# The recurrences of a four-layer kernel: LSTM products in four pieces, a new order of a step, weights split on other engines, and the adaptive part later

## The chip, the cores and the metric

The kernel runs on one core of a Trainium2 chip. Its time is the device time of one execution in microseconds; lower is better. The engines are named as in the profile: PE (TensorE, with PEld for its weight loads), DVE (VectorE), ACT (ScalarE), POOL (GpSimd) and SP (SyncE, which issues most DMAs).

## What is computed

The input x has 8 sequences of 512 positions and 256 features, and every sequence has a condition vector of 256. Four layers are added one after the other, each as a residual:

```
x = x + rnn(x, h0 = cond)                    # h = tanh(x_t Wx + b + h Wh)
x = x + lstm(x, h0 = cond)                   # a = x_t Wx + b + h Wh  (4 x 256 columns)
                                             # i, f, o = sigmoid(a0), sigmoid(a1), sigmoid(a2); g = tanh(a3)
                                             # c = f * c + i * g;  h = o * tanh(c)
x = x + transformer_block(x, cond)           # hyperbolic attention and feed forward,
                                             # shift and scale from ada = cond @ w_ada + b_ada (6 x 256)
x = x + experts(x, cond)                     # 4 experts, the 2 best of a sequence, and a shared one
```

The first two layers are recurrences of 512 steps each. The change lies in them and in what is done beside them: the adaptive product `ada`, and the splitting of the later layers' weights into two parts.

## The kernel before

**The recurrences.** `recurrences` runs both of them in one loop of 520 iterations: in iteration `it` the RNN makes step r = it and the LSTM step l = it - 8, whose input is the RNN's output. PE, ACT and DVE run this loop in the order in which it is written (`manual_schedule`), POOL and SP are scheduled by the framework. Four steps make a quad (G = 4), and s below is the step's place in its quad. All 8 sequences go through a step together, as columns of the stationary operand (8 to 32 of them, as the quad fills up), and the weights are the moving operand, in fp32. The output features lie in four tiles of 32 partitions (Q = 4): `tiles4` issues one product for each, so that a call is four matmuls of the language and, in fp32, eight records of the profile.

**PSUM.** For each of the two alternating quads there are four banks: `pR` holds the RNN's sums (64 columns), and three pieces of `pL` hold the LSTM's 256 columns: 128 columns (f of both halves of the features, i and g of the first half), 64 columns (i and g of the second half), and 64 columns (o). ACT copies the bias into a bank of the coming quad (L391, L402), PE adds the inputs' products (`rnn_inputs`, `lstm_inputs`, spread by `lstm_plan`), and each step adds the products with h (`rnn_mm`, `products`).

**A step of the LSTM** (`lstm_step`): PE makes the first piece, DVE turns it (L476), ACT takes the tanh (L477); likewise the second piece (L481, L482); DVE makes f * c (L483); the third piece is turned (L486) and gets its tanh (L487); DVE scans the first half of the features (L466), ACT takes its tanh (L491), and the same for the second half; DVE multiplies by o (L493) and so writes the h that the next step's products load. Sigmoids are made from tanh.

**A step of the RNN**: `rnn_mm` (PE), a transpose (L434, DVE), a tanh into the slot of h (L435, ACT). In an iteration it stands behind the LSTM's step.

Beside the steps, once per quad: `rnn_add` (L441) adds the RNN's output to x, `turn_x` (L261) turns a quad of x, `lstm_add` (L449) forms the sum that is later stored.

**Weights.** `split_weights` (L178 to L210) makes 44 pieces of 128 x 512: POOL issues the load (L186), copies to fp32r (L188), subtracts (L189) and issues the store of both parts to DRAM (L191, L193). It is called ahead of the loop.

**The adaptive part** (`adaptive`, L499 to L511) makes ada = cond @ w_ada + b_ada in three blocks of 512 columns on PE, spread over the first seven iterations; the results use the banks of the second quad's three pieces. The load of `w_ada` is issued on ACT's queue behind the recurrences' weights (L291).

**After the recurrences** a transformer and experts part follows, in an order that a planner with a cost table makes when the program is built (all its instructions are recorded under L1624). It begins when the last store of the LSTM's output is read back.

Of the kernel before, what the change touches and what calls it, by code (L numbers as in the profile page):

```python
# [11 lines left out]
F32 = mybir.dt.float32  # L12
F32R = mybir.dt.float32r
AF = mybir.ActivationFunctionType
ALU = mybir.AluOpType
# [36 lines left out]
def body(ctx, tc, a, out):  # L52
# [19 lines left out]
    with tc.tile_pool(name="split", bufs=2) as sp:  # L72
        recurrences(
            tc, a, ident, ones, xd, ada_d, condT, ctx, lambda: split_weights(nc, a, sp, sd),
            lambda: constants(nc, a, sp, ident, ones, condT, consts),
        )
# [101 lines left out]
def split_weights(nc, a, pool, sd):  # L178


    G = nc.gpsimd

    def split(n, src):
        name = "_".join(map(str, n))
        raw = pool.tile([P, 2, D], F32, tag="raw", name=f"raw_{name}")
        G.dma_start(raw, src)  # L186
        t = pool.tile([P, 2, 2, D], F32R, tag="parts", name=f"parts_{name}")
        G.tensor_copy(t[:, 0], raw)  # L188
        G.tensor_tensor(t[:, 1], raw, t[:, 0].bitcast(F32), ALU.subtract)  # L189
        if len(n) == 3 and n[0] != E:  # L190
            G.dma_start(sd[n[1:]][n[0] * P : (n[0] + 1) * P], t)  # L191
        else:
            G.dma_start(sd[n], t)  # L193

    def columns(w, q=0):
        return w.rearrange("(c p) g -> p c g", p=P)[:, :, q * D : (q + 1) * D]

    def row_chunks(w, q):
        return w.rearrange("(m p) g -> p m g", p=P)[:, 2 * q : 2 * q + 2, :]

    for n in "qkvo":
        split(n, columns(a[f"L2_cond_w_{n}"]))
    for i in (E, 0, 1, 2, 3):
        w1, w2 = (a[f"L3_cond_sw{k}"] if i == E else a[f"L3_cond_ew{k}"][i] for k in (1, 2))
        for q in range(4):
            split((i, 1, q), columns(w1, q))
            split((i, 2, q), row_chunks(w2, q))


def recurrences(tc, a, ident, ones, xd, ada_d, condT, manual, load_next, constants):  # L210
# [16 lines left out]
    with ExitStack() as ctx:  # L227
# [63 lines left out]
        nc.scalar.dma_start(w_ada, a["L2_cond_w_ada"].rearrange("(c p) g -> p c g", p=P))  # L291
        nc.scalar.dma_start(b_ada, a["L2_cond_b_ada"].rearrange("(o g) -> o g", o=1))
        ada = one.tile([B, 6 * D], F32, name="ada")
        load_next()
# [18 lines left out]
        def set_h(n, q):  # L313
            o = (q % 2) * SET
            return slots[n][:, o + 8 : o + 8 + SET].rearrange("p (u x) -> p u x", x=2 * S + 8)


        bank_R = [ps.tile([P, 512], F32, name=f"pR{i}") for i in range(2)]
        pR = [t[:, : DC * S].rearrange("p (c s) -> p c s", c=DC) for t in bank_R]
        pieces = ((0, 4 * S), (4 * S, 6 * S), (6 * S, 8 * S))  # L320
        bank_L = [[ps.tile([P, 512], F32, name=f"pL{n}{i}") for n in range(3)] for i in range(2)]
        pL = [[bank_L[i][n][:, : hi - lo] for n, (lo, hi) in enumerate(pieces)] for i in range(2)]
# [53 lines left out]
        def open_bank(t, row_of):  # L376
            for j in range(Q):
                nc.tensor.matmul(
                    t[32 * j : 32 * j + 32], lhsT=ones[0:1, :32], rhs=row_of(j), start=True, stop=True, skip_group_check=True
                )  # L380
# [4 lines left out]
        def rnn_inputs(q, i):  # L385

            o = pR[q % 2]
            if i == 0 and q < 2:
                open_bank(o, lambda j: row0.rearrange("p (c j s) -> p c j s", c=DC, j=Q)[:, :, j, :])
            elif i == 0:  # L390
                nc.scalar.copy(flat(o), b0)  # L391
            else:
                k = i - 1
                tiles4(o, XL[:, k, G * q : G * q + G, :].rearrange("p t b -> p (t b)"), w0_cols(wx0, k), False, False)

        def lstm_inputs(q, i, piece):
            lo, hi = pieces[piece]
            o = pL[q % 2][piece]
            if i == 0 and q < 2:
                open_bank(o, lambda j: row1[:, j, lo:hi])  # L400
            elif i == 0:
                nc.scalar.copy(o, b1[:, lo:hi])  # L402
            else:
                k = i - 1
                tiles4(o, XL[:, k, G * q : G * q + G, :].rearrange("p t b -> p (t b)"),
                       lambda j: lw["x"][:, k, j, lo:hi], False, False)


        lstm_plan = [[(0, 0), (0, 1), (0, 2)], [(1, 0), (1, 1)], [(1, 2), (2, 0)], [(2, 1), (2, 2)]]
# [27 lines left out]
        def rnn_add(q):  # L437

            for c in range(DC):
                x = XL[:, c, G * q : G * q + G, :]  # L440
                V.tensor_tensor(x, x, set_h(0, q)[:, :, c * S : c * S + 8], ALU.add)  # L441
# [4 lines left out]
        def lstm_add(q):  # L446
            at = slice(G * q, G * q + G)
            for c in range(DC):
                V.scalar_tensor_tensor(  # L449
                    XT[:, c, :, at].rearrange("p b t -> p t b"),  # L450
                    set_h(1, q)[:, :, c * S : c * S + 8], 0.5, XL[:, c, at, :], ALU.mult, ALU.add,
                )

        def lstm_step(t, between):
# [5 lines left out]
            def products(piece):  # L460
                lo, hi = pieces[piece]
                for k in range(DC):
                    tiles4(pre[piece], h[:, k, : 8 * tt + 8], lambda j: lw["h"][:, k, j, lo:hi], False, tt == G - 1 and k == 1)
# [7 lines left out]
            def tile_of(blocks, tag):  # L471
                return sp.tile([P, blocks, S], F32, tag=tag, name=f"{tag}_{t}")

            products(0)
            f = tile_of(4, "f")
            V.transpose(flat(f), pre[0])  # L476
            nc.scalar.activation(dd[:, 0:4, :, 2], f[:, :, rows], AF.Tanh, scale=0.5)  # L477
            products(1)
            between()
            g = tile_of(2, "g")  # L480
            V.transpose(flat(g), pre[1])  # L481
            nc.scalar.activation(dd[:, 4:6, :, 2], g[:, :, rows], AF.Tanh, scale=0.5)  # L482
            V.scalar_tensor_tensor(dd[:, 2:6:2, :, 3], dd[:, 0:2, :, 2], 1.0, sc_old[:, :, :, 3], ALU.add, ALU.mult)  # L483
            products(2)
            o, to = tile_of(2, "o"), sp.tile([P, DC, B], F32, tag="to", name=f"to_{t}")
            V.transpose(flat(o), pre[2])  # L486
            nc.scalar.activation(to, o[:, :, rows], AF.Tanh, scale=0.5)  # L487
# [11 lines left out]
        def adaptive(i):  # L499
            i, c = divmod(i, DC + 1)  # L500
            cols, pa = slice(512 * i, 512 * (i + 1)), bank_L[1][i][:B]
            if c < DC:
                nc.tensor.matmul(
                    pa, lhsT=condT[:, c, :], rhs=w_ada[:, c, cols], start=(c == 0), stop=False, skip_group_check=True
                )
                return
            nc.tensor.matmul(
                pa, lhsT=ones[0:1, :B], rhs=b_ada[:, cols], start=False, stop=True, skip_group_check=True
            )
            nc.scalar.copy(ada[:, cols], pa)  # L510
            nc.sync.dma_start(ada_d[:, cols], ada[:, cols])  # L511

        b0, b1 = (one.tile([P, n * S], F32, name=f"b{i}") for i, n in enumerate((DC, 8)))
        rnn_inputs(0, 0)
        nc.scalar.copy(b0, flat(pR[0]))
        for i in range(1, 3):
            rnn_inputs(0, i)
        parts = [lambda i=i: adaptive(i) for i in range(3 * (DC + 1))]
        for it in range(T + LAG):
            r, l = it, it - LAG  # L520
            if it == 1:
                turn_rows(XL[:, :, G : G * sizes[0], :], x_first[:, G:, :])
                prepare_bias()
                for piece, (lo, hi) in enumerate(pieces):
                    lstm_inputs(0, 0, piece)
                    nc.scalar.copy(b1[:, lo:hi], pL[0][piece])
            if 1 <= it < LAG:
                for _ in range(-(-len(prepare) // (LAG - it))):
                    prepare.pop(0)()

            def add():
                if r % G == 0 and 0 < r <= T:
                    rnn_add(r // G - 1)

            if l < 0:
                add()
            else:
                if l == 0:
                    for i, piece in sum(lstm_plan, []):
                        if i:  # L540
                            lstm_inputs(0, i, piece)
                lstm_step(l, add)
            if r in (T // 2, T - 3, T - 2):
                fill_constants(bank_R[NQ % 2])
            if r == G:
                fill_constants = constants()
            if 0 < l and l % G == 0:
                lstm_add(l // G - 1)
                if l % P == 0:
                    store(l - P, l)  # L550
            if r < T:
                rnn_mm(r)
                rnn_vec(r)
            if 0 <= l and l // G + 1 < NQ:
                for part in lstm_plan[l % G]:
# [1210 lines left out]
```

## Time and profile before

| | us |
|---|---|
| median of 3 runs | 2729.81 (2729.31 to 2731.14) |
| the profiled execution | 2732.08 |
| its span | 2730.3 |
| PE busy | 2123.2 (78%) |
| PEld busy | 1620.3 (59%) |
| DVE busy | 1957.5 (72%) |
| ACT busy | 1307.5 (48%) |
| POOL busy | 414.6 (15%) |

The span runs from the first to the last instruction of the profiled execution. Busy times are sums over a span with two parts that have different limits, so the share of an engine over the whole says little; stretches of the trace and single steps are read below. Lines such as L370 and L1624 are those of helpers: there the names of the tiles tell groups apart. In the group lines, the number behind x is a count, then come busy time and the mean duration of one in ns, and behind the bar the idle time of the engine just before.

### The profile page before, as it was taken

The page shows a single profiled execution, that of the slowest core. Times are in us where ns is not written, and L with a number is a line of the kernel's source. Part 1 is how long each engine was busy: PE and PEld are TensorE (multiplying, and loading weights), DVE is VectorE, ACT ScalarE, POOL GpSimd, SP SyncE. Part 2 cuts the span into 40 slices and gives each one's busy share as a digit, 9 for nine tenths or more (in the row PEclk, how much of TensorE's full clock was granted, in tenths as well). Part 3 has the DMA queues.
Part 4 walks back from the last instruction along what each step waited for, and adds up shares of the span by engine and source line. Part 5 has one row for each costly group of instructions (what it writes and reads, how often), then busy time and mean ns, then how long its engine had stood idle before and what let it go on. Part 6 is the DMA issues. An engine that isn't in the chain of part 4 may idle for free.

```text
span 2730.3 us, 112042 instructions
## 1 busy us (share of the span) xinstructions
PE 2123.2 (78%) x47067; PEld 1620.3 (59%) x47067; DVE 1957.5 (72%) x8931; ACT 1307.5 (48%) x5047; POOL 414.6 (15%) x467
## 2 busy tenths in 40 slices
PE   5667666766666677766577978889979898999699
PEld 4556656666656566665454444656648475667487
DVE  6776666666666666666565686987877788687884
ACT  2334445454544444444336855455564745564222
POOL 6770000000000000000022332131212222211000
PEclk8568999899999999899888768999989899999799
DMA  7550001000100001000241111433415243243364
GB/s 217 187 184 16 9 5 28 5 12 5 28 5 7 11 5 26 4 5 5 67 155 57 39 60 41 166 130 109 141 66 185 76 145 109 97 139 120 123 208 154
DMA packets 114771, 214.94 MB, mean 79 GB/s; under 512 B 42733, under 2 KB 67888, under 8 KB 114258
## 3 DMA queue, kind: packets, MB, share of 16 engines
q1 hardware_dynamic: 103048, 168.97, 19.0%
q0 software_dynamic: 9856, 34.61, 3.8%
q8 instruction: 369, 6.05, 0.9%
q10 hardware_dynamic: 1362, 4.20, 0.4%
q14 instruction: 136, 1.11, 0.1%
HBM read 167.85 MB, written 39.90 MB: 76 GB/s over the span
## 4 chain that ended last, share of the span: by engine, by line
PE 46%; DVE 30%; ACT 16%; issue 5%; DMA 1%; POOL 1%; SPq 0%; ACTq 0%; DVEq 0%; POOLq 0%
PE pL L370 13%; PE ph L1624 8%; PE py L1624 8%; PE sc L1624 5%; DVE f L476 5%; ACT scan_in L477 5%; PE po L1624 4%; DVE scan_in L483 4%; ACT to L487 4%; DVE slots_h L493 4%; DVE o L486 3%; ACT th L491 2%; PE pf L1624 2%; DVE h L1624 2%; ACT pL L402 1%
## 5 line engine op out<-in xcount | busy, mean ns | idle before, releaser
L370 PE MATMUL pL<-wh,slots_h 128*8 128x64 f32 (+2 forms) x24576 | 608.5, 251 | 409.6 <-DVE slots_h L493 408.5
L370 PEld LDWEIGHTS pL<-wh,slots_h 128*8 128x8 f32 (+1 forms) x24576 | 506.9, 106 | 503.9 <-DVE slots_h L493 492.2
L476 DVE STREAM_TRANSPOSE f<-pL 128x128 f32<-128x128 f32 x512 | 162.1, 317 | 231.8 <-PE pL L370 224.0
L1624 PE MATMUL py<-h,we 128*128 128x512 f32 x1152 | 301.6, 396 | 18.1 <-DVE h L1624 18.1
L1624 ACT ACTIVATE ex<-sc 128x512 f32<-128x512 f32 x512 | 269.0, 612 | 93.5 <-PE sc L1624 91.0
L1624 PE MATMUL ph<-xf,we 128*128 128x512 f32 x1152 | 301.9, 398 | 3.1 <-DVE o L1624 3.1
L477 ACT ACTIVATE scan_in<-f 128x32 f32<-128x32 f32 x512 | 133.8, 261 | 281.0 <-DVE f L476 275.9
L1624 PEld LDWEIGHTS py<-h,we 128*128 128x128 f32 x1152 | 214.6, 189 | 69.7 <-DVE h L1624 24.5
L1624 PEld LDWEIGHTS ph<-xf,we 128*128 128x128 f32 x1152 | 214.8, 190 | 51.8 <-issue 6.7
L370 PE MATMUL pR<-r_L_cond_Wh,slots_h 128*8 128x64 f32 (+3 forms) x8192 | 230.7, 230 | 3.5 <-issue 2.7
L435 ACT ACTIVATE slots_h<-r 128x16 f32<-128x16 f32 x512 | 110.5, 216 | 242.7 <-DVE r L434 242.7
L493 DVE SCALAR_TENSOR_TENSOR slots_h<-to,th 128x8 f32<-128x8 f32 x1024 | 148.7, 172 | 85.2 <-ACT th L491 85.0
L370 PE MATMUL pL<-wx,XL 128*32 128x64 f32 (+1 forms) x6144 | 207.5, 253 | 1.7 <-issue 1.1
L1624 PE MATMUL sc<-q_t,k_t 64*128 64x512 f32 x512 | 172.2, 527 | 28.9 <-ACT ex L1624 25.6
L483 DVE SCALAR_TENSOR_TENSOR scan_in<-scan_in,scan_out 128x16 f32<-128x16 f32 x512 | 125.6, 245 | 94.5 <-ACT scan_in L477 87.1
L466 DVE TENSOR_TENSOR_SCAN scan_out<-scan_in 128x32 f32<-128x32 f32 x1024 | 180.8, 216 | 0.0
L487 ACT ACTIVATE to<-o 128x16 f32<-128x16 f32 x512 | 110.4, 216 | 145.2 <-DVE o L486 127.9
L491 ACT ACTIVATE th<-scan_out 128x8 f32<-128x8 f32 x1024 | 161.4, 204 | 26.1 <-DVE scan_out L466 26.0
L370 PEld LDWEIGHTS pR<-r_L_cond_Wh,slots_h 128*8 128x8 f32 (+3 forms) x8192 | 162.9, 106 | 12.1 <-issue 7.8
L1624 ACT ACTIVATE g<-ph,b 128x512 f32<-128x512 f32 x128 | 87.9, 688 | 170.5 <-PE ph L1624 142.0
L1624 PEld LDWEIGHTS sc<-q_t,k_t 64*128 64x128 f32 x512 | 73.8, 211 | 151.4 <-ACT ex L1624 120.6
L1624 PE MATMUL po<-ex,v 128*32 128x512 f32 x1024 | 162.5, 685 | 0.4 <-ACT ex L1624 0.4
(396 smaller groups left out, 3683.4 us busy)
## 6 DMA issues: line engine op xcount, KB each, us to landing
we<-sde SPq DMA_DIRECT2D x128, 512.0 KB
we<-sd SPq DMA_DIRECT2D x64, 512.0 KB
sde<-parts POOLq DMA_DIRECT2D x32, 512.0 KB, 3.1
raw<-in_L_cond_ew POOLq DMA_DIRECT2D x32, 256.0 KB, 3.5
xT<-xd SPq DMA_DIRECT2D x16, 512.0 KB
sd<-parts POOLq DMA_DIRECT2D x8, 512.0 KB, 3.7
xd<-XT SPq DMA_DIRECT2D x4, 1024.0 KB
xtd<-x SPq DMA_DIRECT2D x8, 512.0 KB
```

The costliest lines, as they stand in the source:

```text
L370: nc.tensor.matmul(out[32 * j : 32 * j + m], lhsT=lhsT, rhs=rhs_of(j), start=start, stop=stop, skip_group_check=True)
L402: nc.scalar.copy(o, b1[:, lo:hi])
L435: nc.scalar.activation(slot_h(0, t + 1), r[:, :, 8 * tt : 8 * tt + 8], AF.Tanh)
L466: V.tensor_tensor_scan(sc[:, c].rearrange("p b s -> p (b s)"), dd[:, 2 + 2 * c].rearrange("p b s -> p (b s)"), dd[:, 3 + 2 * c].rearrange( ...
L476: V.transpose(flat(f), pre[0])
L477: nc.scalar.activation(dd[:, 0:4, :, 2], f[:, :, rows], AF.Tanh, scale=0.5)
L483: V.scalar_tensor_tensor(dd[:, 2:6:2, :, 3], dd[:, 0:2, :, 2], 1.0, sc_old[:, :, :, 3], ALU.add, ALU.mult)
L486: V.transpose(flat(o), pre[2])
L487: nc.scalar.activation(to, o[:, :, rows], AF.Tanh, scale=0.5)
L491: nc.scalar.activation(th[c], sc[:, c, :, 3], AF.Tanh)
L493: V.scalar_tensor_tensor(out[:, c], to[:, c], 1.0, th[c], ALU.add, ALU.mult)
L1624: r = f(*args, **kw)
```

## The change

In the recurrences:

- The LSTM's sums lie in four pieces of 64 columns, one bank each: f of both halves, i and g of the first half, i and g of the second, o. `pR` moves into columns 64 to 128 of the fourth piece's bank. Each step issues the products of all four pieces in a row.
- DVE turns the four pieces one by one, and ACT takes one tanh per piece; f * c stands behind the third transpose, o's transpose behind f * c.
- An iteration begins with the RNN's transpose and tanh, and its products for the coming step stand at the end of the iteration. `rnn_add` (now one instruction), `turn_x` and `lstm_add` stand at s = 0, 1 and 2, between the RNN's transpose and the LSTM's first. ACT's bias copies stand two by two at s = 0 and 1, one ahead of the step's tanhs and one behind them.
- The weights are split in 88 halves of pieces, from the LSTM's third quad on, one per quad: ACT copies (`hi`) at the end of s = 2, DVE subtracts (`lo`) at s = 3. Loads and stores stay on POOL's queue.
- The load of `w_ada` is issued on POOL's queue at l = 4, and `ada` is made in six blocks of 256 columns in the LSTM's quads 95 to 100, in unused columns of the pieces' banks.

```diff
-        bank_R = [ps.tile([P, 512], F32, name=f"pR{i}") for i in range(2)]
-        pR = [t[:, : DC * S].rearrange("p (c s) -> p c s", c=DC) for t in bank_R]
-        pieces = ((0, 4 * S), (4 * S, 6 * S), (6 * S, 8 * S))
-        bank_L = [[ps.tile([P, 512], F32, name=f"pL{n}{i}") for n in range(3)] for i in range(2)]
+        NP = 4
+        bank_L = [[ps.tile([P, 512], F32, name=f"pL{n}{i}") for n in range(NP)] for i in range(2)]
+        pieces = tuple((2 * S * n, 2 * S * (n + 1)) for n in range(NP))
+        pL = [[bank_L[i][n][:, : 2 * S] for n in range(NP)] for i in range(2)]
+        pR = [bank_L[i][NP - 1][:, 2 * S : 4 * S].rearrange("p (c s) -> p c s", c=DC) for i in range(2)]
...
+    def hi(self):
+        i, c = self.jobs[0]
...
+        self.nc.scalar.copy(self.parts[i][:, 0, c], self.raw[i][:, c])
+
+    def lo(self):
+        i, c = self.jobs.pop(0)
+        t, n = self.parts[i], self.pieces[i][0]
+        self.nc.vector.tensor_tensor(t[:, 1, c], self.raw[i][:, c], t[:, 0, c].bitcast(F32), ALU.subtract)
+        if c == 0:
+            return
...
+        self.load(i + 2)
...
-            products(0)
-            f = tile_of(4, "f")
-            V.transpose(flat(f), pre[0])
-            nc.scalar.activation(dd[:, 0:4, :, 2], f[:, :, rows], AF.Tanh, scale=0.5)
-            products(1)
-            between()
...
+            for piece, (lo, hi) in enumerate(pieces):
+                for k in range(DC):
+                    tiles4(pre[piece], h[:, k, : 8 * tt + 8], lambda j: lw["h"][:, k, j, lo:hi], False, tt == G - 1 and k == 1)
+            for piece in range(3):
+                nc.scalar.activation(dd[:, 2 * piece : 2 * piece + 2, :, 2], turned(piece), AF.Tanh, scale=0.5)
             V.scalar_tensor_tensor(dd[:, 2:6:2, :, 3], dd[:, 0:2, :, 2], 1.0, sc_old[:, :, :, 3], ALU.add, ALU.mult)
...
+            to = sp.tile([P, DC, B], F32, tag="to", name=f"to_{t}")
+            nc.scalar.activation(to, turned(3), AF.Tanh, scale=0.5)
...
+            if r < T:
+                rnn_vec(r)
...
+            if s == 0 and 0 < r <= T:
+                rnn_add(rq - 1)
+            elif s == 1 and next_r:
+                turn_x(rq + 1)
+            elif s == 2 and l > 0:
+                if lq > 0:
+                    lstm_add(lq - 1)
...
+            elif s == 3 and split:
+                weights_split.lo()
+
+            if lq >= 1 and s < 2:
+                start_piece(lq + 1, 2 * s, next_l, next_r)
...
+            if l >= 0:
+                lstm_step(l)
+
+            if s < 2:
+                start_piece(lq + 1, 2 * s + 1, lq >= 1 and next_l, rq >= 1 and next_r)
+            if s == 2 and split:
+                weights_split.hi()
+
+            plan = ([(0, 0), (0, 1)], [(1, 0), (1, 1), (2, 0)], [(2, 1), (3, 0), (3, 1)], [])[s]
+            if next_l:
+                for part in plan:
+                    lstm_inputs(lq + 1, *part)
+            if s == 3 and next_r:
+                for k in range(DC):
+                    rnn_inputs(rq + 1, k)
+            if r + 1 < T:
+                rnn_mm(r + 1)
+            if ada_i is not None and s in (0, 2):
+                if s == 0:
+                    ada_row(ada_i)
+                ada_products(ada_i, s // 2)
...
+            if l == G:
+                V.memset(w_ada[:, 0, :1], 0.0)
+                nc.gpsimd.dma_start(w_ada, a["L2_cond_w_ada"].rearrange("(c p) g -> p c g", p=P))
...
-        for it in range(T + LAG):
-            r, l = it, it - LAG
...
-                lstm_step(l, add)
...
-            if r < T:
-                rnn_mm(r)
-                rnn_vec(r)
```

## The prediction

> **What bounds the kernel now.** I read the slices of the page first, then busy time by stretch, then the two stretches' instructions, then one step in order of time, last the chain of waits of the start.
>
> ```profile
> span 2730.3 us, 112042 instructions
> POOL 6770000000000000000022332131212222211000
> PEclk8568999899999999899888768999989899999799
> ```
>
> The recurrences fill the first half (their last result is at 1348.6 us); POOL works only in the first three of 40 slices there, and just there the TensorE clock is low. Stretches (PE, PEld, DVE, ACT, POOL busy, then clock, DMA share, GB/s):
>
> ```profile
> 60.00:200.00 140.00, 85.30 (x2700) 73.42 (x2692) 107.46 (x352) 44.95 (x234) 101.47 (x130) 0.62 0.56 186
> 200.00:1340.00 1140.00, 793.56 (x37333) 704.75 (x37333) 765.70 (x4904) 561.15 (x3268) 5.54 (x10) 0.96 0.05 11
> ```
>
> One instruction of L483 runs in each LSTM step, so its record counts steps (min/median/max ns, first and last start):
>
> ```profile
> L483 DVE SCALAR_TENSOR_TENSOR scan_in<-scan_in,scan_out x42: 140/561/1911, 33.2 to 203.9; 128x16 f32<-128x16 f32 x42
> L483 DVE SCALAR_TENSOR_TENSOR scan_in<-scan_in,scan_out x470: 146/190/196, 207.2 to 1347.6; 128x16 f32<-128x16 f32 x157
> ```
>
> 42 steps take (207.2 - 33.2) / 42 = 4.143 us each while POOL splits weights, 470 take (1347.6 - 207.2) / 469 = 2.432 after. The order of time in the slow phase shows why:
>
> ```profile
> 103.82 1.79 DVE L466 TENSOR_TENSOR_SCAN scan_out<-scan_in 128x32 f32<-128x32 f32 x2
> 104.12 1.28 POOL L189 TENSOR_TENSOR parts<-raw,parts 128x512 fp32r<-128x512 f32 x1
> 105.52 0.33 ACT L491 ACTIVATE th<-scan_out 128x8 f32<-128x8 f32 x2 [1.38 <-DVE scan_out L466]
> ```
>
> Two scans that end together after 0.30 us elsewhere last until POOL's instruction is over. Row by row between 60 and 206 us, 14 scans that overlap POOL's TENSOR_TENSOR have a median of 1890 ns; 37 that overlap only a POOL DMA issue have 188.
>
> An undisturbed step is a latency chain; no engine is full:
>
> ```profile
> 800.29 1.09 PE L370 MATMUL pL<-wh,slots_h 128*32 128x128 f32 x48 [0.62 <-DVE slots_h L493]
> 801.00 0.32 DVE L476 STREAM_TRANSPOSE f<-pL 128x128 f32<-128x128 f32 x1 [0.49 <-PE pL L370]
> 801.41 0.27 ACT L477 ACTIVATE scan_in<-f 128x32 f32<-128x32 f32 x1 [0.65 <-DVE f L476]
> 801.71 0.19 DVE L483 SCALAR_TENSOR_TENSOR scan_in<-scan_in,scan_out 128x16 f32<-128x16 f32 x1 [0.24 <-ACT scan_in L477]
> 801.82 0.24 DVE L486 STREAM_TRANSPOSE o<-pL 128x64 f32<-128x64 f32 x1
> 801.98 0.30 DVE L466 TENSOR_TENSOR_SCAN scan_out<-scan_in 128x32 f32<-128x32 f32 x2
> 802.21 0.31 ACT L491 ACTIVATE th<-scan_out 128x8 f32<-128x8 f32 x2
> 802.45 0.28 DVE L493 SCALAR_TENSOR_TENSOR slots_h<-to,th 128x8 f32<-128x8 f32 x2 [0.17 <-ACT th L491]
> 802.67 0.89 PEld L370 LDWEIGHTS pL<-wh,slots_h 128*8 128x8 f32 x48 [0.72 <-DVE slots_h L493]
> ```
>
> 0.71 us from the first product to the first transpose, then 1.67 back to the next first product: 2.38. The start, from the chain of waits:
>
> ```profile
> 2.91 15.67 DMA w_ada<-in_L_cond_w_ada
> 18.62 1.98 PE pL L503 x3
> ```
>
> The adaptive products stand in PE's queue and wait for their weights; the first LSTM product is at 31.48.
>
> **The change part by part.** The profiled execution took 2732.1 us (its span 2730.3, 1.8 around it), 2.3 above the median 2729.8. The instruction order of the changed build is the same, on all five engines, in everything after the recurrences, so the 1381.7 us from 1348.6 to the end stay. The sum is what the recurrences lose.
>
> *Weights split off POOL.* POOL keeps DMA issues only, so the long scans go: 42 x (4.143 - 2.432) = **-71.9 us**. The clock comes back with it: the short steps ran at 0.96. What is added: 88 ScalarE copies and 88 VectorE subtractions of 128x256, one pair every four steps, for which the nearest rows are the cast k_s (414 ns) and kh (418 ns). The copy stands behind a step's last tanh, the subtraction behind the RNN transpose of the next step, while PE makes products: DVE idles 0.49 us there (row 801.00), and the copy's end is covered by ScalarE's wait before the first gate. In the new step below the subtraction may run from 0.29 to 0.71 with the next DVE instruction free to start at 0.63; the f transpose is due at 0.60, the ig transpose at 0.82. Taken as 0; bounds 0 and 88 x (0.414 + 0.418) = 73 us if all of it lay bare; a gain is excluded, as it is added work. The DMA issues (0.73 and 0.57 us each) block only POOL; loads run two pieces ahead, 17 us.
>
> *Four pieces.* In the rows of single instructions a group of four 128-column products follows the last by 109 ns, of 64 columns by 56 ns, so PE's streaming is unchanged (16 groups x 56 ns against 4 x 109 + 8 x 56), but f is ready sooner and its transpose is 64 wide (243 ns, as L486). The new step, from k=0's weight load, with the latencies of the rows (PE to DVE 0.07, DVE to ACT 0.03 or 0.09 where ACT waits for two semaphores as at L477, ACT to DVE 0.03, DVE to PE 0.05): the load for k=1 waits for the second half of h, at 0.185. Ten groups later (f's last two, ig's eight) the third piece is ready: 0.79. Then 0.07, transpose 0.24, 0.09, tanh 0.235, 0.03, scan 0.19, 0.04, th 0.21, 0.03, h 0.17, 0.05: 2.16 from one k=1 load to the next. The f chain arrives earlier (transpose at 0.60, tanh 0.94 to 1.17, f*c at 1.21, o's transpose 1.32, first scan 1.48), so ig's second half now ends last, as L476 did before. Steps before run 2.388 on average where the clock stays full, 2.432 with the windows in which it halves; I keep that surplus, round 2.16 to 2.15 for products that follow a wait a little faster, and take **2.19**: 512 x (2.432 - 2.19) = **-123.9 us**. Bounds: 2.10 (h's first half sets the pace, no clock dips) to 2.31 (half the gain lost).
>
> *A rule against the split*: the Trainium skill, "TensorE: Matmul & The Clock Gate", section "Wait — 56ns, not 53.3ns?", says that starts of matmuls never come closer than about 25 ns, however few columns. An estimate by it: a step has 25 groups of four records (16 LSTM, 4 RNN, 4 and 1 inputs), 100 x 25 ns = 2.5 us, PE would be the bound and the step gain nothing: 2533 + 512 x 0.31 = 2692. The trace has the 64-column products in these column tiles 56 ns per four, 14 ns apart; I take the trace.
>
> *Shared bank.* The RNN's sums now lie in the bank of o's piece; in the built order the RNN products wait for o's transpose, and o's products for the RNN transpose. No row shows such a wait. By the step above: o's transpose ends at 1.56, the RNN's four groups are done at 2.05, their transpose is due at 2.21: nothing. Behind that wait PE has only the next step. If it came late, the cost is at most 0.1 us on three steps of four, 38 us; a gain is excluded (a wait only delays). Taken as 0.
>
> *Other moves.* rnn_add, turn_x, lstm_add, one per step in the same gap (0.2 to 0.3 us): 0. Bank copies: as many, two before and two after ScalarE's tanhs: 0. rnn_mm at a step's end: its result is wanted only at the next step's start.
>
> *Adaptive part later.* Start: after the row set-up at about 16.5 us (with the transposes and bias products as before) seven RNN steps of 1.25 us (r to r 1.02 to 1.20 at 26 to 29 us before), the first input products at half clock: LSTM from about 26.5, not 31.48: **-5** (2 to 8). Later: 128x512 cost 0.86 us of PE each before (two passes 0.43 apart), 256 columns 0.43; in six quads, 0.86 us behind the RNN products of one step, 0.43 of another; PE has 0.3 us left there: 6 x (0.56 + 0.13) = **+4.1**. Its load (1.5 MB) is issued by POOL at l = 4, ninety quads early. SP gets six ada_d stores (0.29 us issue) for three, and x loads behind them are sixteen quads ahead.
>
> Sum -71.9 - 123.9 - 5 + 4.1 = -196.7: 2732.1 - 196.7 = 2535.4 profiled, 2533 as a median.
>
> **The rivals.**
> *A cold clock* (the other side). At 60 to 200 us the clock was 0.62 though no pause of PE reached 3.3 us. The same page's Part 1 has it halve after an idle window of about 3.4 us; the row shows that thin work is enough. Should the new spacing fall under it, a group takes 0.112 us (1.91 us for 48 records at 101.67, 1.08 at 800.29), 25 of them 2.80 us: PE-bound. The rest brings 73 us, so the total turns slower from a mean step of 2.432 + 73 / 512 = 2.574, that is 63% of steps cold; all cold gives 2533 + 512 x 0.61 = 2845. Against it: PE is denser than before (1.4 us in 2.19), and at 1.4 in 2.43 it had 0.96. 3%.
> *Half of the step's gain*: split work or bank waits on the path, 2.31: 2533 + 61 = 2594. The slack of 0.1 us around the RNN transpose speaks for it. 17%.
> *PE's floor*, above: 2692. 3%.
> *The DVE slowness follows the transfers, not POOL's arithmetic*: then 88 of the LSTM steps keep a 1.7 us longer scan, 2533 + 150 = 2683. The 188 ns rows speak against it. 3%.
>
> **How the numbers follow.** My forecast, 2533, with its own bounds, holds 74%. The range 2490 to 2590 takes the fast end (2.10 a step, -46) and nearly all of the half-gain case. A measurement of this kernel can tell 0.2% (5.5 us). Slower needs the cold clock: 3%; the same 1%; faster 96%.
>
> **What would show it.** After: scans at 188 ns from the start; POOL idle but for issues; first LSTM products at 26 to 27 us; L483's successor 2.15 to 2.2 us apart; the scan of ig's second half the last arrival; recurrences over at about 1152; 1382 us behind them. Wrong if the step stays at 2.3 or more, if the clock is below 0.9, or if the subtraction or the RNN transpose delays the f transpose.

## The result, and the profile after

The changed kernel is slower: 2946.47 us (2944.28 to 2952.18, 4 runs) against 2730.47 (2729.31 to 2741.92) of the kernel before on the same chip, a ratio of 1.0784 (95% interval 1.0751 to 1.0817). 2533 was predicted. The profiled execution took 2944.28 us, with a span of 2942.5.

The page of the changed kernel, the slices that answer to those shown of before:

```profile
span 2942.5 us, 134830 instructions
...
POOL 0000000000000000000001223113121212221100
PEclk9999999999999999999998767798999999999899
```

POOL issues DMAs and does nothing else through the recurrences, and the clock is at nine tenths or more there from the first slice on. The program has grown by some 22,800 instructions. The same two stretches as before:

```profile
60.00:200.00 140.00, 89.65 (x4768) 72.48 (x4765) 91.83 (x551) 73.92 (x395) 7.62 (x12) 1.00 0.13 39
200.00:1340.00 1140.00, 747.66 (x37822) 608.43 (x37825) 727.83 (x4326) 585.30 (x3106) 48.00 (x78) 0.97 0.13 36
```

The first stretch shows all that was meant for it: POOL's busy time fell from 101.47 to 7.62 us and the clock rose from 0.62 to 1.00. The second carries the surprise: PE and DVE are less busy than before (PE 747.66 us for 793.56, DVE 727.83 for 765.70), ACT hardly more (585.30 for 561.15, with the split's copies), PE made almost the same number of products (37822 against 37333), though a step now has 25% more of them, and no engine is fuller for it. The step's counter, now at L504 (min/median/max ns, first and last start):

```profile
L504 DVE SCALAR_TENSOR_TENSOR scan_in<-scan_in,scan_out x512: 144/177/194, 28.4 to 1557.1; 128x16 f32<-128x16 f32 x171
```

The recurrences begin 4.8 us earlier and end 209.5 us later. That is (1557.1 - 28.4) / 511 = 2.992 us a step. Behind the last of these the rest takes 1385.4 us (1382.7 before): the whole loss is in the steps. The spread of the steps tells more than their mean. Taken from the starts of that instruction between 300 and 1200 us, the fastest steps take 2.15 us, which is the step that the prediction worked out ahead of its allowance for the clock, but the median is 3.07 and one in twenty takes over 4.04. A fast one, in order of time:

```profile
839.08 0.15 DVE L504 SCALAR_TENSOR_TENSOR scan_in<-scan_in,scan_out 128x16 f32<-128x16 f32 x1
...
840.06 1.00 PEld L395 LDWEIGHTS pL<-wh,slots_h 128*32 128x32 f32 x64 [0.25 <-DVE slots_h L512]
840.31 0.42 DVE L221 TENSOR_TENSOR parts<-raw,parts 128x256 fp32r<-128x256 f32 x1
840.65 0.67 DVE L490 STREAM_TRANSPOSE turned<-pL 128x64 f32<-128x64 f32 x3
841.25 0.19 DVE L504 SCALAR_TENSOR_TENSOR scan_in<-scan_in,scan_out 128x16 f32<-128x16 f32 x1
```

From 839.08 to 841.25 is 2.17 us, and this step even holds a subtraction of the split (L221): it lies where the prediction put it, and f's transpose begins 0.59 us after the first weight load (0.60 predicted). The waits of PE between 300 and 1200 us (line, releaser: us in total, times, longest) name what the other steps have. After:

```profile
PE pL L395 <- issue: 231.3, 218, 3.3
PE pL L395 <- DVE slots_h L512: 47.5, 125, 1.2
```

Before:

```profile
PE pL L370 <- DVE slots_h L493: 266.8, 345, 1.3
PE pR L370 <- issue: 4.0, 12, 0.7
PE pL L370 <- issue: 1.8, 7, 0.4
```

Before, PE waited for h, once in nearly every step, as at the end of a latency chain. After, it waits for h in fewer than half the steps, and stands still 231 us for nothing that the profile shows ("issue"). One such stop, in the chain of waits and in the order of time:

```profile
802.01 0.38 PE pL L395 x10
802.39 1.42 issue
```

```profile
802.32 0.28 DVE L512 SCALAR_TENSOR_TENSOR slots_h<-to,th 128x8 f32<-128x8 f32 x2 [0.17 <-ACT th L510]
803.82 0.26 PE L395 MATMUL pL<-r_L_cond_Wh,slots_h 128*32 128x64 f32 x3 [1.42 <-issue]
```

PE makes 10 of the 16 products of an RNN step, stops for 1.42 us in the middle of a group that has no wait in it, and goes on; the new h was written at 802.60 and found nobody. What a stop in the middle of a group can lack is the instruction itself. The transfers between 300 and 1200 us have a queue for that (packets, MB, share of 16 engines); before, then after:

```profile
q8 instruction: 232, 3.80, 1.8%
```

```profile
q8 instruction: 232, 3.80, 1.7%
```

The two kernels fetch the same number of packets in 900 us, one per 3.88 us, though one makes 25% more products per step. A packet is 3.80 MB / 232 = 16.4 KB. PE's records (matmuls and weight loads) in the window are 59184 before and 59313 after, some 256 to a packet. (The Trainium skill, "Advanced Engine Details and Errata", section "ISA Cache", speaks of cache lines of 16 KB that hold 256 instructions; the trace agrees.) Hence 160 / 256 x 3.88 = 2.43 us a step before and 200 / 256 x 3.88 = 3.03 after, the mean steps of that window, 2.431 and 3.034. This is counting and no evidence: whether packets pace the steps or steps the packets, the product is the same. That both kernels come to 3.88 is chance: the kernel before takes a packet as its steps use it up, as is shown next.

The trace itself tells the two apart. Number all of PE's instructions in it by their start (products, weight loads and those of its sequencer) and sort the pauses of PE over 0.25 us between 300 and 1200 us by that number modulo 256. In the changed kernel 219 of 275 stand at one and the same place of the 256, with 234.5 us of the 268.4, so at 219 of 232 packets PE stopped; of those over 1 us it is 118 of 119. In the kernel before that same place has 11 pauses with 5.4 us. A wait for a result, or for a bank, has no reason to come back every 256 instructions, across steps of 160 to 200.

The times fit. The changed kernel has 109 stops of PE longer than 1 us between 300 and 1100 us. The time from the end of the last q8 packet to PE's first record behind the stop is 1.39 us in the median, and 1.24 to 1.56 from the 5th to the 95th percentile. For moments drawn at random it is 1.97, and 0.20 to 3.83. PE goes on a fixed time after a packet has come in. And from such a restart to the start of the next transfer it is 1.17 us in the median, the transfer takes 1.02, then come the 1.39: 3.58 in sum, where PE was through a packet's 256 instructions in 2.81 (median). It looks as if the next packet were asked for only when PE is some way into the last one, so that the limit is a round trip and not a bandwidth; that is read from the order of times and was not tested.

### The profile page after: what moved, and what is told of

Same layout as the page of the kernel before. It is cut to its first block, busy times and chain, and to the rows that moved or that the text cites. A ratio compares the mean times of both kernels' runs of the same rounds, so it can differ in the third digit from the quotient of the medians.

```text
span 2942.5 us, 134830 instructions
## 1 busy us (share of the span) xinstructions
PE 2221.8 (76%) x57341; PEld 1640.0 (56%) x57341; DVE 2032.9 (69%) x9406; ACT 1473.7 (50%) x5653; POOL 334.3 (11%) x381
## 4 chain that ended last, share of the span: by engine, by line
PE 46%; DVE 23%; issue 17%; ACT 11%; DMA 1%; SPq 1%; POOL 1%; ACTq 0%; DVEq 0%; POOLq 0%
PE pL L395 18%; PE ph L1687 5%; PE py L1687 5%; DVE turned L490 5%; PE sc L1687 5%; PE po L1687 4%; ACT scan_in L503 4%; DVE h L1687 3%; ACT to L506 2%; DVE slots_h L512 2%; ACT th L510 2%; PE pf L1687 2%; ACT ex L1687 1%; DVE r L464 1%; SPq L275 1%
## 5 line engine op out<-in xcount | busy, mean ns | idle before, releaser
L395 PE MATMUL pL<-wh,slots_h 128*8 128x64 f32 x32768 | 668.8, 226 | 330.3 <-issue 225.4
L395 PEld LDWEIGHTS pL<-wh,slots_h 128*8 128x8 f32 x32768 | 534.8, 102 | 445.7 <-issue 265.3
L490 DVE STREAM_TRANSPOSE turned<-pL 128x64 f32<-128x64 f32 x2048 | 469.4, 245 | 337.3 <-PE pL L395 323.0
L503 ACT ACTIVATE scan_in<-turned 128x16 f32<-128x16 f32 x1536 | 333.8, 231 | 370.6 <-DVE turned L490 285.2
L395 PE MATMUL pL<-r_L_cond_Wh,slots_h 128*8 128x64 f32 (+3 forms) x8192 | 248.7, 227 | 119.9 <-issue 75.3
L395 PE MATMUL pL<-wx,XL 128*32 128x64 f32 x8192 | 225.4, 226 | 59.8 <-issue 58.4
L395 PEld LDWEIGHTS pL<-r_L_cond_Wh,slots_h 128*8 128x8 f32 (+3 forms) x8192 | 159.6, 102 | 178.0 <-issue 86.1
L464 DVE STREAM_TRANSPOSE r<-pL 128x64 f32<-128x64 f32 x512 | 125.5, 245 | 142.5 <-PE pL L395 140.5
L395 PEld LDWEIGHTS pL<-wx,XL 128*32 128x32 f32 x8192 | 172.1, 114 | 69.0 <-issue 63.8
L510 ACT ACTIVATE th<-scan_out 128x8 f32<-128x8 f32 x1024 | 182.3, 213 | 2.2 <-DVE scan_out L494 1.2
```

The costliest lines, as they stand in the source:

```text
L395: nc.tensor.matmul(out[32 * j : 32 * j + m], lhsT=lhsT, rhs=rhs_of(j), start=start, stop=stop, skip_group_check=True)
L464: V.transpose(flat(r), flat(pR[q % 2]))
L490: V.transpose(flat(o), pre[piece])
L503: nc.scalar.activation(dd[:, 2 * piece : 2 * piece + 2, :, 2], turned(piece), AF.Tanh, scale=0.5)
L510: nc.scalar.activation(th[c], sc[:, c, :, 3], AF.Tanh)
```

## The experiments

Theory A: PE's instructions come in packets of 256 at some 3.8 us each, and the step is bound by its number of PE records. Theory B: the new order of a step, or the bank shared by the RNN's sums and o's piece, makes PE wait. Theory C: what counts is PE's own time for the products, on the path or off it.

**Old pieces in the new order (e1), and two pieces (e2).** Both keep the new order, the shared bank, the split on ACT and DVE and the late adaptive part. e1 cuts the 256 columns as the kernel before did (160 records a step), e2 into two pieces of 128 (f and the first ig; the second ig and o; 120 records); the bias copies and input products are dealt out to the steps to suit. e2's core:

```diff
-        NP = 4
+        NP = 2
-        pieces = tuple((2 * S * n, 2 * S * (n + 1)) for n in range(NP))
+        pieces = ((0, 4 * S), (4 * S, 8 * S))
...
-            for piece in range(3):
-                nc.scalar.activation(dd[:, 2 * piece : 2 * piece + 2, :, 2], turned(piece), AF.Tanh, scale=0.5)
+            nc.scalar.activation(dd[:, 0:4, :, 2], turned(0), AF.Tanh, scale=0.5)
+            go = turned(1)
+            nc.scalar.activation(dd[:, 4:6, :, 2], go[:, 0:2], AF.Tanh, scale=0.5)
...
-            nc.scalar.activation(to, turned(3), AF.Tanh, scale=0.5)
+            nc.scalar.activation(to, go[:, 2:4], AF.Tanh, scale=0.5)
```

e1 was expected so: 

> The changed kernel with the LSTM's sums in the old three pieces (128, 64, 64 columns); new order of a step, shared bank of RNN and last piece, split on ACT and DVE, and later adaptive part all stay. Theory A (TensorE's instructions arrive in packets of 16 KB, 256 instructions, one per about 3.8 us at best; four pieces need 200 instructions a step, three need 160): 160/256 x 3.8 = 2.38 us, so steps of 2.38 to 2.45, issue pauses of PE nearly gone, total about 2650. Theory B (the new order or the wait on the shared bank holds PE up): steps stay near 2.99 and the total near 2940.

e2 was expected so: 

> The changed kernel with two pieces of 128 columns (f and first half of ig; second half of ig and o): 120 instructions a step. Theory A: 120/256 x 3.8 = 1.78 us, far under the latency chain, which I work out at 2.32 us (second transpose 128 wide, ready 0.08 us later than the 64 wide third one); no issue pauses; total about 2606. Theory B: as the changed kernel or worse, 2940.

Measured: e1 2690.70 us, 0.9842 of before (0.9819 to 0.9864); e2 2632.66 us, 0.9634 (0.9606 to 0.9662). e2 has half as many records of the LSTM's products as the changed kernel and is 314 us faster than it; of all versions run that compute the whole it is the fastest. Its q8 packets and PE's stops in the same 900 us:

```profile
q8 instruction: 179, 2.93, 1.4%
```

```profile
PE pL L395 <- issue: 2.1, 1, 2.1
```

Fewer packets, one per 5.03 us, and a single stop: the queue has slack, and 94 of 100 steps take 2.34 to 2.44 us. B falls as the cause of the loss, since its suspects are all in e1 and e2; that it costs a little is not excluded (see the last group). e1 is 40 us slower than A expected: its median step is 2.36, its mean 2.50, and it still stops:

```profile
PE pL L395 <- issue: 49.3, 96, 2.6
```

**More instructions in the kernel before (e3, e4).** One or two spare calls per RNN step, into unused columns of `pR`'s bank, change nothing else but that these columns are set to zero once: 176 and 192 records a step, that is 8 or 16 more products, which stream in 0.11 or 0.22 us (56 ns per group of four).

```diff
+                for _ in range(2):
+                    spare = bank_R[r // G % 2][:, 64:128].rearrange("p (c s) -> p c s", c=DC)
+                    tiles4(spare, slot(0, r)[:, 0, : 8 * (r % G) + 8], w0_cols(wh0, 0), False, False)
```

One call was expected so: 

> The kernel before with one more group call of small products per RNN step, into unused columns of the RNN's bank, at a place where PE idles: 16 more PE instructions a step (176), 0.11 us of PE time. The added sums are read by nobody. Theory A: 176/256 x 3.8 = 2.61 us a step in the 470 undisturbed steps, +0.18 each, total about 2815. Theory C (PE time or a per-record floor is the bound, not the arrival of instructions): 0 to +0.11 us a step, total 2732 to 2784.

Two calls were expected so: 

> The same with two added group calls per step: 192 PE instructions a step, 0.22 us of PE time. Theory A: 192/256 x 3.8 = 2.85 us a step, +0.42 each, total about 2930. Theory C: 0 to +0.22 us a step, total 2732 to 2837.

Measured in one run each: 2804.92 and 2904.09 us, mean steps 2.59 and 2.82. The stops of e4, and its packets:

```profile
PE pR L370 <- issue: 112.4, 94, 4.1
PE pL L370 <- issue: 95.8, 117, 1.7
```

```profile
q8 instruction: 239, 3.92, 1.8%
```

The second call makes the mean step 0.23 us longer, twice the 0.11 us that its products stream, and most of both calls' cost stands under issue: (112.4 + 95.8) / 319 steps of that window is 0.65 us a step, some of it in time that PE would else have waited for h. The packets stand at 239 in both runs, 3.77 us each, and PE stopped for 158 and 197 of them, at the same place of the 256: this is the supply at its limit, and the old order with its own banks runs into it as well. C gave at most 2784 and 2837. The second run lies 67 us above that and the first 21, where seven runs of the kernel before spread over 16: C falls, by the second above all.

**One part alone (e7).** The kernel before with only the split moved to ACT and DVE (`hi` at the end of a step with s = 2, `lo` behind the RNN's transpose at s = 3):

```diff
-            tc, a, ident, ones, xd, ada_d, condT, ctx, lambda: split_weights(nc, a, sp, sd),
+            tc, a, ident, ones, xd, ada_d, condT, ctx, SplitWeights(nc, a, sp, sd),
...
+            if l >= 2 * G and weights_split.jobs:
+                if l % G == 3:
+                    weights_split.lo()
+                elif l % G == 2:
+                    weights_split.hi()
```

> The kernel before with one part of the change: the weights split by ACT and DVE beside the steps (copy at the end of an LSTM step with s = 2, subtraction at s = 3 behind the RNN's transpose and tanh), three pieces, order and adaptive part as before. My prediction's term for this part was -72: 2730 - 72 = 2658, steps from 60 to 206 us at 2.43 in place of 4.14. Theory A leaves that term whole but adds the split's transfers over 360 steps: in the changed kernel a step took 3.05 us with them and 2.94 without, so up to 0.1 us a step where PE stands at the edge of its supply (160 records): 2658 to 2695. Rival: the copies and subtractions lie bare on the step, 88 x (0.41 + 0.42) = 73 us: 2730, no gain.

Measured: 2671.14 us, 0.9774 of before (0.972 to 0.9828), some 62 us gained. The step's counter (now L503) and the first stretch:

```profile
L503 DVE SCALAR_TENSOR_TENSOR scan_in<-scan_in,scan_out x512: 150/190/196, 32.9 to 1287.8; 128x16 f32<-128x16 f32 x171
```

```profile
60.00:200.00 140.00, 96.16 (x4580) 85.78 (x4573) 97.99 (x613) 72.72 (x412) 8.90 (x14) 0.95 0.15 46
```

The recurrences end 59.8 us earlier, the slow phase is gone, and the rival that the work lies bare falls. The 12 us that lack from 72 are in the later steps: 2.465 us on average from 300 to 1200 us, 2.431 before, and (2.465 - 2.431) x 360 is 12. Its stops are 34.7 us in that window against 5.8, at 49 packets against 11. The split's transfers (some 40 GB/s) go beside the instruction packets. That they delay the packets fits, and wasn't tested by itself; the changed kernel's steps (3.04 us from 300 us on while they run, 2.94 after the last) can't tell, since the clock differs too (0.96 and 0.98).

**Fewer instructions with four pieces (e6, e9, e8).** From the changed kernel, e6 takes the LSTM's input products away from the second quad on (168 records), e9 also the RNN's from the third (160), e8 also half of the RNN's products with h (144). So they leave out part of the computation. The four pieces, the order, the shared bank and the split stay in all three.

```diff
-            if next_l:
+            if next_l and lq < 0:
...
-            if s == 3 and next_r:
+            if s == 3 and next_r and rq < 0:
...
-            for k in range(DC):
+            for k in (1,):
                 tiles4(pR[q % 2], h[:, k, : 8 * tt + 8], w0_cols(wh0, k), False, tt == G - 1 and k == 1)
```

e6: 

> The changed kernel with the LSTM's input products left out from the second quad on (the part left out of the computation): 168 records of PE per step in place of 200; four pieces, the new order, the shared bank and the split weights are all kept. Theory A (instructions reach PE in packets of 256, one per some 3.83 us): 168 / 256 x 3.83 = 2.51 us a step in place of 2.99, so 2944 - 512 x 0.48 = about 2700, and the pauses called issue between 300 and 1200 us fall from 231 to some 50 us. Theory B (the new order or the shared bank makes PE wait): these products stand behind the step's chain, so the step stays near 2.99 and the time at 2944; at most the 0.3 us of their streaming goes, 2790.

e9: 

> Run e6 with the RNN's input products left out too (from the third quad on; RNN's products with h kept): 160 records in a clean step of 2.15 us, 74 a us, as in the run with one spare call per step (176 in 2.37), whose step rose by 0.22. Theory A by the rate that four pieces ask for: 2.37 to 2.45, total about 2640; A by the mean count alone (160 x 3.83 / 256): 2.39, the same. If e6's step of 2.75 has a second cause that goes with the order or the bank: 2.65 to 2.75, total 2770 to 2810.

e8: 

> Run e6 with more left out: the RNN's input products (from the third quad on) and the first half (k = 0) of the RNN's products with h; these parts of the computation are left out, the LSTM's four pieces with all their products, the order, the shared bank and the split stay. 144 records of PE per step: in a clean step of 2.15 us that is 67 records a us, what the kernel before asks for (160 in 2.37). Theory A: pauses as rare as before, the step 2.15 to 2.25, total 2944 - 512 x (2.99 - 2.20) = about 2540. Theory B (the new order or the shared bank holds PE up, which e6's 2811 leaves possible): the step stays near e6's 2.75, total about 2810.

Measured: e6 2810.87 us (2803.16 to 2826.11, 4 runs), e9 2728.83 and e8 2622.77 (one run each). The stops called issue, from 300 to 1200 us, of e6 and e8 in this order (e9 has 89.0 us in 150):

```profile
PE pL L395 <- issue: 123.5, 155, 2.8
```

```profile
PE pL L395 <- issue: 28.8, 67, 1.7
```

e6 by itself would not have decided: it lies 111 us above A's number and near B's lower one. e8 decides: the median step is 2.17 us and the mean 2.36, where B said 2.75, so with the order and the shared bank as they were, fewer instructions take most of the loss away. But each of the three is some 80 to 110 us slower than A expected. All runs in one table, from 300 to 1200 us; the clean step is the median of the steps with no stop over 0.1 us at a packet and no window in which the granted clock was one half, "asked" is records by clean step, and the last column is the share of packets for which PE stopped over 0.25 us. (Mean step and time per packet are one measurement: their ratio is records / 256.)

| kernel | records per step | clean step, us | asked, per us | mean step, us | us per packet | stopped for |
|---|---|---|---|---|---|---|
| two pieces (e2) | 120 | 2.35 | 51 | 2.38 | 5.03 | 1% |
| before | 160 | 2.37 | 68 | 2.43 | 3.88 | 5% |
| split alone (e7) | 160 | 2.37 | 68 | 2.47 | 3.93 | 21% |
| three pieces (e1) | 160 | 2.36 | 68 | 2.50 | 3.96 | 33% |
| before + 1 call (e3) | 176 | 2.37 | 74 | 2.59 | 3.77 | 66% |
| before + 2 calls (e4) | 192 | 2.38 | 81 | 2.82 | 3.77 | 82% |
| e8 | 144 | 2.16 | 67 | 2.36 | 4.15 | 22% |
| e9 | 160 | 2.16 | 74 | 2.55 | 4.04 | 62% |
| e6 | 168 | 2.16 | 78 | 2.75 | 4.17 | 73% |
| after | 200 | 2.15 | 93 | 3.03 | 3.88 | 94% |

In the old order and in that of four pieces alike, the mean step and the share of packets that PE stopped for grow with what is asked. Two packets never start closer than 3.2 us, which would be 79 records a us; in the long run the rate was never above 256 / 3.77 = 68. What lies near it loses to stops, and what lies above it is paced by it.

At about the same number asked, the four pieces lose some 0.15 us a step more than the old order (e8 0.20 above its clean step, before 0.06). The clock is little of that in e8 (the steps with half clock add 0.06 to its mean, 0.04 to that of before) and more in e6 (0.09, and 0.01 in e4). Two other things show in the traces and stay unseparated. The first is a wait of PE ahead of the RNN's products, which share their bank with o's piece; in e8, where the kernel before has no such line:

```profile
PE pL L395 <- ACT scan_in L503: 110.4, 228, 0.5
```

It is 0.29 us a step, and the clean step of 2.16 holds with it. The second is that the next packet comes later where PE waits: from a stop's restart to the next transfer it is 1.14 us (median) where PE runs on, and 1.87 (e8) to 2.03 (e6) where it pauses over 0.1 us in between, which is so in 94 of e6's 157 stops and in none of e4's 197. So a wait inside a packet seems to be paid again at its end. A run with four pieces and a bank of its own for the RNN is missing.

## Why the prediction was wrong, point by point

**The step that failed** is in the part on four pieces: "so PE's streaming is unchanged (16 groups x 56 ns against 4 x 109 + 8 x 56)", and with it the term "512 x (2.432 - 2.19) = -123.9 us". The streaming within a step is unchanged indeed, but the records are not: 96 for the LSTM's products with h became 128, and 24 for its inputs 32. The prediction put the cost of bringing 40 more instructions a step to PE at nothing. At 68 records a us, the most that any run had in the long run, the 200 of a step take 2.94 us. In the place of -123.9 the runs show 511 x (2.992 - 2.432) = **+286**. With this term replaced, the sum comes to 2732.1 - 71.9 + 286 - 5 = 2941.2 (the adaptive part lies within the 2.992); the profiled execution took 2944.3, and 2.7 of the rest lie behind the recurrences. This is bookkeeping with measured steps; that the cause is the supply rests on the stops and the experiments.

**The sentence before it that let it through** is "no engine is full". PE's busy share of 70% said nothing on it: neither its array nor, as yet, the supply of its instructions was full, but the supply had almost no room left. The page before showed the queue as a line with 0.9% of the DMA engines' time, easily passed over. Counted over the window, the kernel before already took a packet per 3.88 us, where no run came under 3.77. Its surplus of 0.06 us over the chain, which the prediction put down to the clock, was no sign of that: 40 of 369 steps had half clock and took 2.77, which is 0.04, and the 24 with a stop at a packet took 2.37 like the others.

**The rule that I weighed and set aside.** The floor of about 25 ns per matmul (the Trainium skill, "TensorE: Matmul & The Clock Gate", section "Wait — 56ns, not 53.3ns?") gave 2.5 us a step and 2692; I took the 14 ns between products of column tiles, which is right within a burst. Over many steps a packet of 256 records holds 128 matmuls, 3.8 us / 128 = 30 ns each. So the rival had the right quantity (the number of records) by luck, with another mechanism: within a step there is no such floor, as the 64 weight loads of the fast step above in 1.00 us show (16 ns each). Its total was still 254 us short.

**The clean step**, 2.16 worked out, is right: the fastest steps take 2.15. (The terms as printed add up to 2.145.) **The split off POOL**, -71.9, is right in kind: the long scans are gone from the first stretch on, and alone it brought 62 of 72 us. Its copies and subtractions cost nothing that can be seen, but 12 us came with it that I had at 0, in later steps with more stops at packets. **The start**: -4.8 (predicted -5). **The adaptive part later**: in the steps of its quads the changed kernel takes 3.06 us, their neighbours 2.95, so about 24 x 0.11 = 3 us (4.1 predicted); with two pieces 24 x 0.29 = 7. **The shared bank**: put at 0. It is not the cause of the loss, since e1, e2 and e8 have it too; a part in the 0.15 us that the four pieces lose beyond the old order is not excluded. **After the recurrences**: 1385.4 for 1382.7, as foreseen.

**The rivals.** A cold clock was the only case on the slower side, and it isn't what happened: the clock was 1.00 and 0.97 in the two stretches above. Half of the step's gain and the DVE's slowness by transfers fall, too. The case that came, a supply of instructions at its edge, was not among them.

## What to carry to other kernels

Count the instructions that a change makes an engine issue, not only the time that they stream. Smaller pieces shorten a latency chain, but each brings its own matmuls and weight loads; on this kernel some 68 PE records a us was what arrived in the long run, and stops began near it. Look for "issue" ahead of PE in the waits and for the spacing of instruction packets in the stretch, before the change as well as after: this kernel sat at 3.88 us per packet and had no room for more. Whether a pause is a wait for instructions can be told from one trace: see whether the pauses come back at the same place of every 256 of the engine's instructions.

## What the hardware showed that I had not expected

- PE's instructions arrive during the run, in packets of 16.4 KB (256 instructions), never less than 3.2 us apart and 3.8 to 4.2 apart on average in the runs where PE stopped for most of them; the transfer of one lasts about 1.0 us, and PE goes on 1.39 us after its end. In the changed kernel 219 of 275 pauses stand at one place of the 256.
- A kernel at 68 records a us stood at the edge without a sign in any busy share: 16 more records a step (0.11 us of streaming) made its mean step 0.16 us longer, 32 (0.22 us) made it 0.39 longer.
- With the split's transfers of some 40 GB/s beside it, the kernel before had stops at 49 packets in 900 us in place of 11, and 0.03 us more a step; whether the transfers delay the packets is not settled.
